# Mixture-of-experts rows turned by the DMA engines instead of TensorE, as two 16-bit halves

## The chip, the cores and the metric

The kernel runs on one core of a Trainium2 chip. A core has TensorE (matrix products and transposes; its sequence of weight loads is listed apart, as PEld), VectorE (DVE), ScalarE (ACT), GpSimd (POOL) and SyncE (SP), which here does nothing but issue transfers; 16 DMA engines carry all transfers. The engines run their own instruction streams in order and wait for each other through semaphores. On-chip data lies in SBUF (128 partitions); results of TensorE go to PSUM and are copied out by another engine. The metric is the device time of the whole program in microseconds (us), as the median of several runs.

## The reference

The input x is 2 x 2048 tokens of 512 float32 values. With xn the layer-normalised x, the result is x + s * g, where

```python
xn = _layernorm(x, axis=-1)
s = _L0_attn_ref(xn, ...)       # normalise again, causal attention of one head, key size 512, plus xn
g = _silu(_L0_ffn_ref(xn, ...)) # 8 experts, the best 2 per token
# inside _L0_ffn_ref, with xf = xn as (4096, 512):
scores = xf @ gate_w.T + gate_b + bias
top_scores, top_idx = jax.lax.top_k(scores, TOP_K)
gates = jax.nn.softmax(top_scores, axis=-1)
h = jax.nn.silu(jnp.einsum('td,ehd->teh', xf, w1) + b1)   # hidden size 352
y = jnp.einsum('teh,edh->ted', h, w2) + b2
out = jnp.einsum('ted,te->td', y, comb)  # comb: the two gates of a token
```

## The kernel before, in words

The work is written in four stages; a scheduler then orders the instructions of each engine ahead of time, and pools of buffers decide when a buffer may be used again.

First stage, lines 139 to 283: eight blocks of four token tiles (128 tokens each). `prepare(b)` loads x, takes its statistics on VectorE, makes the twice-normalised z (line 224) and, in place, the normalised x (line 229), and stores the latter as rows of `xn_d` in DRAM (line 232). TensorE transposes z; VectorE and ScalarE make kT and zT from it, and eight columns of gate scores follow. `project(b)`, three blocks later, makes q and v and stores them through four staging buffers (lines 273 and 283). The x buffer has two copies, so the load of block b+1 needs the store of block b-1 to be done.

Second, `route()`: the top two experts of each token, and a list of slots. Each expert's tokens are padded to whole slot tiles of 128 rows; there are 71 of them (NS). `toki` has the token of each slot, `eidi` the expert of each slot tile. The last three projections run on TensorE beside and behind it.

Third, the expert stage, lines 482 to 573, which the change is about. For slot tile i: `fetch(i)` gathers 128 rows of 2 KB from `xn_d` by an indirect transfer of GpSimd (line 503). `turn(i)` transposes the four 128x128 blocks on TensorE into PSUM (line 513), and VectorE copies them to xT (line 515). `up(i)` multiplies with the expert's w1 (line 527, eight instructions), ScalarE copies h out (line 532), `turn_h(i)` transposes h (line 540) and ScalarE applies silu with the bias (line 542). `down(i)` multiplies with w2 (line 552, six instructions), VectorE copies y out (line 557), and SyncE stores it to `y_d` (line 558). The loop puts them in this order:

```python
for i in range(NS):
    if i + AHEAD < NS:
        fetch(i + AHEAD)
    up(i)
    if i + 1 < NS:
        turn(i + 1)
    if i:
        down(i - 1)
    turn_h(i)
```

Fourth, lines 577 to 710: causal attention over the stored q, k, v, the gather of each token's two rows of `y_d`, the gate and the output.

All plain transfers named here are issued by SyncE, in order: an issue that waits holds up those behind it. The built program also lets each of them wait for the completion of the one eight places before it.

Of the kernel before, what the change touches and what calls it, by code (L numbers as in the profile page):

```python
# [10 lines left out]
F32 = mybir.dt.float32  # L11
BF16 = mybir.dt.bfloat16
I32 = mybir.dt.int32
AF = mybir.ActivationFunctionType
ALU = mybir.AluOpType
AX = mybir.AxisListType
# [3 lines left out]
P = 128  # L20
# [5 lines left out]
def gated_attention_moe(  # L26
# [26 lines left out]
    nc = tc.nc  # L53
    B, S, D = x.shape
    E, _, H = w1_t.shape
    KEY = o_proj.shape[0]
    NT = B * S // P
    BT = 4
# [3 lines left out]
    ND = D // P  # L62
# [10 lines left out]

    dram = ctx.enter_context(tc.tile_pool(name="dram", bufs=1, space=DRAM))
    xn_d = dram.tile([NT * P, D], F32, name="xn_d")
    y_d = dram.tile([NS * P, D], F32, name="y_d")
    kt_d = [dram.tile([P, ND, TB], F32, name=f"kt_d{b}") for b in range(NB)]
    qt_d = [dram.tile([P, ND, TB], F32, name=f"qt_d{b}") for b in range(NB)]
    v_d = [dram.tile([P, BT, D], F32, name=f"v_d{b}") for b in range(NB)]
    xn_rows = xn_d.rearrange("(n p) d -> p n d", p=P)  # L80
    y_rows = y_d.rearrange("(n p) d -> p n d", p=P)

    const = ctx.enter_context(tc.tile_pool(name="const", bufs=1))

    ident = const.tile([P, P], F32, name="ident")
# [5 lines left out]
        out=keep, in_=keep, compare_op=ALU.is_ge, fill=-HUGE,  # L91
# [38 lines left out]
    psum = lambda st, **k: st.enter_context(tc.tile_pool(space=PSUM, **k))  # L130
# [70 lines left out]
    def prepare(b):  # L201

        if b + 1 < NB:
            load(b + 1)
        xt = xin.pop(b)
        mv = sm.tile([P, BT, 2], F32, name=f"mv_{b}", tag="mv")  # L210
        for t in range(BT):
            st = sm.tile([P, 6], F32, name=f"st_{b}_{t}", tag="st")
            nc.vector.bn_stats(st, xt[:, t, :])
            nc.vector.bn_aggr(mv[:, t, :], st)
        va = sm.tile([P, BT, 2], F32, name=f"va_{b}", tag="va")
        nc.vector.tensor_scalar(va[:, :, 0:1], mv[:, :, 1:2], EPS, None, ALU.add)
        nc.vector.tensor_scalar(
            va[:, :, 1:2], mv[:, :, 1:2], 1.0 + EPS, EPS * EPS, ALU.mult, ALU.add
        )
        rs = rstd_of(sm, va, 2, "a")  # L220
        zs = []
        for t in range(BT):
            z = zp.tile([P, D], F32, name=f"z_{b}_{t}", tag="z")
            nc.vector.tensor_scalar(
                z, xt[:, t, :], mv[:, t, 0:1], rs[:, t, 1:2], ALU.subtract, ALU.mult
            )
            zs.append(z)
        for t in range(BT):
            nc.vector.tensor_scalar(
                xt[:, t, :], xt[:, t, :], mv[:, t, 0:1], rs[:, t, 0:1], ALU.subtract, ALU.mult  # L230
            )
        nc.sync.dma_start(out=xn_rows[:, ts(b, BT), :], in_=xt)

        ratio = sm.tile([P, BT], F32, name=f"ratio_{b}", tag="ratio")
        nc.vector.tensor_tensor(ratio, va[:, :, 1], rs[:, :, 1], ALU.mult)
        nc.vector.tensor_tensor(ratio, ratio, rs[:, :, 0], ALU.mult)

        zT = ztp.tile([P, ND, TB], F32, name=f"zT_{b}", tag="zT")
        kT = kp.tile([P, ND, TB], F32, name=f"kT_{b}", tag="kT")
        for c in range(ND):  # L240
            pt = ps_t.tile([P, TB], F32, name=f"pz_{b}_{c}", tag="pt")
            for t in range(BT):
                nc.tensor.transpose(pt[:, ts(t, P)], zs[t][:, ts(c, P)], ident)  # L243
            nc.scalar.copy(zT[:, c, :], pt)
            nc.vector.tensor_scalar(
                kT[:, c, :], pt, gam[:, c : c + 1], bet[:, c : c + 1], ALU.mult, ALU.add
            )
        nc.sync.dma_start(out=kt_d[b], in_=kT)
        kts[b] = kT
        pg = ps_g.tile([P, BT, E], F32, name=f"pg_{b}", tag="pg")  # L250
        for t in range(BT):
            for c in range(ND):
                nc.tensor.matmul(  # L253
                    pg[:, t, :], lhsT=zT[:, c, ts(t, P)], rhs=gw[:, c, :],
                    start=(c == 0), stop=(c == ND - 1),
                )
        nc.vector.tensor_tensor(
            sc[:, :, ts(b, BT)], pg.rearrange("p t e -> p e t"),
            ratio.unsqueeze(1).to_broadcast([P, E, BT]), ALU.mult,
        )  # L260
# [219 lines left out]


    with ExitStack() as st:
        xsp = st.enter_context(tc.tile_pool(name="xsp", bufs=4))
        xtp = st.enter_context(tc.tile_pool(name="xtp", bufs=2))
        hp = st.enter_context(tc.tile_pool(name="hp", bufs=2))
        yp = st.enter_context(tc.tile_pool(name="yp", bufs=3))
        htp = st.enter_context(tc.tile_pool(name="htp", bufs=1))
        hts = []
        for i in range(3):
            ht = htp.tile([P, NH, P], F32, name=f"ht_{i}", tag=f"ht_{i}")  # L490
            nc.gpsimd.memset(ht[HL : HL + 1, NH - 1, :], 1.0)
            hts.append(ht)
        stage_a.close()
        ps_x = psum(st, name="ps_x", bufs=2)
        ps_h = psum(st, name="ps_h", bufs=2)
        ps_ht = psum(st, name="ps_ht", bufs=2)
        ps_y = psum(st, name="ps_y", bufs=2)

        xss, xts, hs, experts = {}, {}, {}, {}

        def fetch(i):
            xs = xsp.tile([P, D], F32, name=f"xs_{i}", tag="xs")
            nc.gpsimd.indirect_dma_start(  # L503
                out=xs, out_offset=None, in_=xn_d,
                in_offset=bass.IndirectOffsetOnAxis(ap=toki[:, i : i + 1], axis=0),
            )
            xss[i] = xs

        def turn(i):
            xs = xss.pop(i)  # L510
            px = ps_x.tile([P, ND, P], F32, name=f"px_{i}", tag="px")
            for c in range(ND):
                nc.tensor.transpose(px[:, c, :], xs[:, ts(c, P)], ident)  # L513
            xT = xtp.tile([P, ND, P], F32, name=f"xT_{i}", tag="xT")
            nc.vector.tensor_copy(xT, px)  # L515
            xts[i] = xT

        def up(i):
            ev = nc.values_load(
                eidi[0:1, i : i + 1], engines=[mybir.EngineType.PE], min_val=0, max_val=E - 1,  # L520
                skip_runtime_bounds_check_because="a sum of E comparisons, the first of them true, less one",
            )
            experts[i] = ev
            xT = xts.pop(i)
            ph = ps_h.tile([P, H], F32, name=f"ph_{i}", tag="ph")
            for c in range(ND):
                nc.tensor.matmul(  # L527
                    ph, lhsT=xT[:, c, :], rhs=w1[:, bass.ds(ev, 1), c, :].rearrange("p o h -> p (o h)"),
                    start=(c == 0), stop=(c == ND - 1),
                )  # L530
            h = hp.tile([P, H], F32, name=f"h_{i}", tag="h")
            nc.scalar.copy(h, ph)
            hs[i] = h

        def turn_h(i):
            h = hs.pop(i)
            ht = hts[i % 3]
            pht = ps_ht.tile([P, NH, P], F32, name=f"pht_{i}", tag="pht")
            for c, (h0, hn) in enumerate(HCH):
                nc.tensor.transpose(pht[:hn, c, :], h[:, h0 : h0 + hn], ident)  # L540
            for c, (h0, hn) in enumerate(HCH):
                nc.scalar.activation(  # L542
                    ht[:hn, c, :], pht[:hn, c, :], AF.Silu, bias=b1sel[:hn, c, i : i + 1]
                )

        def down(i):
            ht = hts[i % 3]
            ev = experts.pop(i)
            py = ps_y.tile([P, D], F32, name=f"py_{i}", tag="py")
            for c, (_, hn) in enumerate(HCH):  # L550
                k = hn + 1 if c == NH - 1 else hn
                nc.tensor.matmul(  # L552
                    py, lhsT=ht[:k, c, :], rhs=w2[:k, bass.ds(ev, 1), c, :].rearrange("p o d -> p (o d)"),
                    start=(c == 0), stop=(c == NH - 1),
                )
            y = yp.tile([P, D], F32, name=f"y_{i}", tag="y")
            nc.vector.tensor_copy(y, py)  # L557
            nc.sync.dma_start(out=y_rows[:, i, :], in_=y)

        AHEAD = 3  # L560
        for i in range(AHEAD):
            fetch(i)
        turn(0)
# [9 lines that stand above are left out]
        down(NS - 1)  # L573
# [181 lines left out]
```

## Time and profile before

| what | value |
|---|---|
| time, median of 3 runs | 1321.16 us (1318.1 to 1328.13) |
| span of the profiled execution | 1319.4 us |
| first gather issued | 280.6 us |
| first transpose of slot tiles (line 513) | 324.3 us |
| last store of y issued | 732.7 us |
| stores of y, 256 KB each, issue to landing | 2.0 us |
| gathers, 256 KB each, issue to landing (median) | 3.3 us |
| first and last load of x | 1.7 and 127.0 us |

The profile is one execution. Busy time of an engine counts its instructions other than waits and issues of transfers; a group line gives, for one line of the kernel and one kind of instruction, output<-input, the count, busy time in us, mean ns of one, and the idle time of that engine before it with what ended most of it. Busy times of TensorE's groups overlap a little, since its instructions are pipelined. The chain follows the work that ended last back through what released it.

### The profile page before, as it was taken

To read this page: it belongs to the slowest core of one execution; us is meant where nothing else is said; L and a number is where in the kernel's file an instruction comes from. 1 tells how busy PE (TensorE), PEld (TensorE's weight loads), DVE (VectorE), ACT (ScalarE), POOL (GpSimd) and SP (SyncE) were. 2 spreads that over 40 slices of the span, in tenths; PEclk is the share of its full clock that TensorE was granted. 3 is DMA by queue.
4 is the path that set the end of the run, shared out by engine and by line. 5 is a ranking of instruction groups with operands and counts; after the bars stand their busy time and mean duration, and the time that the engine had idled before them with its cause. 6 is when DMAs were issued, how large, how long until landed. Compare 5 with 4: busy or idle time off the path is not lost.

```text
span 1319.4 us, 11878 instructions
## 1 busy us (share of the span) xinstructions
PE 1231.6 (93%) x3973; PEld 647.2 (49%) x3973; DVE 558.4 (42%) x1046; ACT 231.6 (18%) x593; POOL 261.3 (20%) x258
## 2 busy tenths in 40 slices
PE   6899999999999999999999478999999988899997
PEld 2565555444555555555555234444444434444443
DVE  2666223940222222222222395655444786554521
ACT  1222212111222222222222111111111011111010
POOL 0000000010111111111110364423112464321101
PEclk9899999999999999999999788999999999999999
DMA  9697332122322222222221883323114644121000
GB/s 349 218 358 279 128 128 88 72 96 99 119 94 96 89 95 89 96 94 90 90 95 64 326 295 104 122 69 111 41 40 177 237 128 137 59 68 48 24 9 16
DMA packets 68490, 162.84 MB, mean 123 GB/s; under 512 B 8968, under 2 KB 13064, under 8 KB 64336
## 3 DMA queue, kind: packets, MB, share of 16 engines
q1 hardware_dynamic: 52432, 116.71, 24.4%
q0 software_dynamic: 10800, 35.40, 8.7%
q10 hardware_dynamic: 5200, 9.98, 2.2%
q8 instruction: 33, 0.54, 0.2%
q14 instruction: 25, 0.20, 0.1%
HBM read 101.51 MB, written 60.56 MB: 123 GB/s over the span
## 4 chain that ended last, share of the span: by engine, by line
PE 52%; issue 22%; DVE 13%; POOL 6%; DMA 4%; SPq 1%; ACT 1%; POOLq 0%; ACTq 0%; DVEq 0%
PE py L552 14%; PE ph L527 13%; PE pv L277 8%; PE pq L267 8%; DVE e L622 7%; POOL o L693 3%; PE px L513 2%; POOL g L623 2%; PE pg L253 2%; PE pht L540 2%; DVE g L615 1%; DVE g L614 1%; PE pz L243 1%; ACT e L620 1%; DMA x<-in_x_dram 1%
## 5 line engine op out<-in xcount | busy, mean ns | idle before, releaser
L685 PE MATMUL po<-v,pT 128*128 128x512 f32 x544 | 253.9, 615 | 43.5 <-DVE pT L677 33.3
L640 PE MATMUL ps<-k,q 128*128 128x512 f32 (+3 forms) x640 | 246.0, 537 | 6.3 <-issue 6.3
L552 PE MATMUL py<-w,ht 128*128 (+1 forms) x426 | 194.8, 593 | 0.5 <-ACT ht L542 0.5
L685 PEld LDWEIGHTS po<-v,pT 128*128 128x128 f32 x544 | 102.5, 196 | 170.5 <-issue 108.1
L527 PE MATMUL ph<-w,xT 128*128 x568 | 179.9, 460 | 0.4 <-DVE xT L515 0.4
L640 PEld LDWEIGHTS ps<-k,q 128*128 128x128 f32 x640 | 118.4, 195 | 123.6 <-issue 115.9
L503 POOL DMA_INDIRECT xs<-xn_d,toki x71 | 67.4, 950 | 423.8 <-PE px L513 349.5
L515 DVE COPY xT<-px 128x512 f32<-128x512 f32 x71 | 49.0, 692 | 217.1 <-PE px L513 217.1
L267 PE MATMUL pq<-kT,wqk 128*128 128x512 f32 x256 | 125.0, 626 | 0.0
L527 PEld LDWEIGHTS ph<-w,xT 128*128 128x128 f32 x568 | 102.3, 190 | 45.7 <-DVE xT L515 0.6
L277 PE MATMUL pv<-wvo,kT 128*128 128x512 f32 x256 | 115.1, 596 | 0.0
L552 PEld LDWEIGHTS py<-w,ht 128*128 128x128 f32 (+1 forms) x426 | 75.6, 191 | 68.8 <-issue 51.2
L557 DVE COPY y<-py 128x512 f32<-128x512 f32 x71 | 49.1, 692 | 137.8 <-PE py L552 137.8
L622 DVE RECIPROCAL e<-e 128x512 f32<-128x512 f32 x32 | 107.1, 3346 | 0.4
L542 ACT ACTIVATE ht<-pht,b1sel 128x128 f32<-128x128 f32 (+1 forms) x213 | 62.0, 362 | 198.4 <-PE pht L540 198.4
L693 POOL TENSOR_TENSOR o<-o,g 128x512 f32<-128x512 f32 x32 | 40.5, 1266 | 258.7 <-DVE o L692 254.9
L656 ACT ACTIVATE pr<-ps,nm 128x512 f32<-128x512 f32 (+2 forms) x80 | 49.0, 620 | 219.2 <-DVE nm L651 216.2
L608 POOL DMA_INDIRECT yg<-y_d,posi x64 | 68.9, 1076 | 67.5 <-DMA y_d<-y 36.9
L277 PEld LDWEIGHTS pv<-wvo,kT 128*128 128x128 f32 x256 | 46.9, 190 | 51.0 <-issue 50.9
L692 DVE SCALAR_TENSOR_TENSOR o<-po,ri,xn 128x512 f32<-128x512 f32 x32 | 23.6, 737 | 106.1 <-PE po L685 106.1
L267 PEld LDWEIGHTS pq<-kT,wqk 128*128 128x128 f32 x256 | 47.5, 200 | 42.6 <-issue 42.4
L620 ACT ACTIVATE e<-g 128x512 f32<-128x512 f32 x32 | 20.1, 629 | 263.3 <-DVE g L615 252.7
(128 smaller groups left out, 937.4 us busy)
## 6 DMA issues: line engine op xcount, KB each, us to landing
y_d<-y SPq DMA_DIRECT2D x71, 256.0 KB, 2.0
x<-in_x_dram SPq DMA_DIRECT2D x32, 256.0 KB, 6.3
xn_d<-x SPq DMA_DIRECT2D x8, 1024.0 KB, 5.5
kt_d<-kT SPq DMA_DIRECT2D x8, 1024.0 KB, 4.6
qt_d<-q SPq DMA_DIRECT2D x32, 256.0 KB, 2.4
v_d<-v SPq DMA_DIRECT2D x32, 256.0 KB, 2.3
xn<-xn_d SPq DMA_DIRECT2D x32, 256.0 KB, 2.7
xo<-in_x_dram SPq DMA_DIRECT2D x32, 256.0 KB, 4.6
```

The costliest lines, as they stand in the source:

```text
L267: nc.tensor.matmul(pq, lhsT=wqk[:, c, ts(r, P)], rhs=kT[:, c, :], start=(c == 0), stop=(c == ND - 1),)
L277: nc.tensor.matmul(pv, lhsT=kT[:, c, ts(t, P)], rhs=wvo[:, c, :], start=(c == 0), stop=(c == ND - 1),)
L503: nc.gpsimd.indirect_dma_start(out=xs, out_offset=None, in_=xn_d, in_offset=bass.IndirectOffsetOnAxis(ap=toki[:, i : i + 1], axis=0),)
L527: nc.tensor.matmul(ph, lhsT=xT[:, c, :], rhs=w1[:, bass.ds(ev, 1), c, :].rearrange("p o h -> p (o h)"), start=(c == 0), stop=(c == ND - 1),)
L542: nc.scalar.activation(ht[:hn, c, :], pht[:hn, c, :], AF.Silu, bias=b1sel[:hn, c, i : i + 1])
L552: nc.tensor.matmul(py, lhsT=ht[:k, c, :], rhs=w2[:k, bass.ds(ev, 1), c, :].rearrange("p o d -> p (o d)"), start=(c == 0), stop=(c == NH - 1),)
L557: nc.vector.tensor_copy(y, py)
L608: nc.gpsimd.indirect_dma_start(out=y, out_offset=None, in_=y_d, in_offset=bass.IndirectOffsetOnAxis(ap=posi[k][:, n : n + 1], axis=0),)
L622: nc.vector.reciprocal(e, e)
L640: nc.tensor.matmul(ps[:, :w], lhsT=qts[b][:, c, ts(t, P)], rhs=kts[first + j][:, c, :w], start=(c == 0), stop=(c == ND - 1),)
L685: nc.tensor.matmul(po, lhsT=turned[j][:, ts(i, P)], rhs=vs[first + j][:, i, :], start=(j == 0 and i == 0), stop=(j == len(widths) - 1 and ...
L693: nc.gpsimd.tensor_tensor(o, o, g, ALU.mult)
```

## The change: the transpose moves from TensorE to the DMA engines

The DMA engines can transpose[...], and the rows are float32. So a float32 row is treated as 512 pairs of 16-bit halves. In the first stage GpSimd splits each normalised tile into a row of 512 low halves and 512 high halves, and SyncE stores these rows in a second DRAM tensor, `xh_d`, beside `xn_d`, which the fourth stage still reads. The expert stage gathers from `xh_d`; SyncE then issues a transposing transfer from SBUF to SBUF, 128 rows of 1024 halves to 8 blocks of 128x128, and VectorE's copy, which before took the result from PSUM, puts the two halves of every value side by side again in xT. No bit is lost, so xT is the same as before. Four TensorE transposes per slot tile and their PSUM buffers go. The gather and its buffers are one deeper: 5 buffers for the rows and 5 for the transposed halves, and four tiles of look-ahead in place of three. The rest of the program is the same.

```diff
--- before.py
+++ after.py
@@ -11,6 +11,7 @@
 F32 = mybir.dt.float32
 BF16 = mybir.dt.bfloat16
 I32 = mybir.dt.int32
+U16 = mybir.dt.uint16
 AF = mybir.ActivationFunctionType
 ALU = mybir.AluOpType
 AX = mybir.AxisListType
@@ -73,11 +74,14 @@
 
     dram = ctx.enter_context(tc.tile_pool(name="dram", bufs=1, space=DRAM))
     xn_d = dram.tile([NT * P, D], F32, name="xn_d")
+
+    xh_d = dram.tile([NT * P, 2 * D], U16, name="xh_d")
     y_d = dram.tile([NS * P, D], F32, name="y_d")
     kt_d = [dram.tile([P, ND, TB], F32, name=f"kt_d{b}") for b in range(NB)]
     qt_d = [dram.tile([P, ND, TB], F32, name=f"qt_d{b}") for b in range(NB)]
     v_d = [dram.tile([P, BT, D], F32, name=f"v_d{b}") for b in range(NB)]
     xn_rows = xn_d.rearrange("(n p) d -> p n d", p=P)
+    xh_rows = xh_d.rearrange("(n p) d -> p n d", p=P)
     y_rows = y_d.rearrange("(n p) d -> p n d", p=P)
 
     const = ctx.enter_context(tc.tile_pool(name="const", bufs=1))
@@ -230,6 +234,14 @@
                 xt[:, t, :], xt[:, t, :], mv[:, t, 0:1], rs[:, t, 0:1], ALU.subtract, ALU.mult
             )
         nc.sync.dma_start(out=xn_rows[:, ts(b, BT), :], in_=xt)
+        for t in range(BT):
+            xh = zp.tile([P, 2, D], U16, name=f"xh_{b}_{t}", tag="xh", bufs=2)
+            nc.gpsimd.tensor_copy(
+                xh, xt[:, t, :].bitcast(U16).rearrange("p (d h) -> p h d", h=2)
+            )
+            nc.sync.dma_start(
+                out=xh_rows[:, b * BT + t, :], in_=xh.rearrange("p h d -> p (h d)")
+            )
 
         ratio = sm.tile([P, BT], F32, name=f"ratio_{b}", tag="ratio")
         nc.vector.tensor_tensor(ratio, va[:, :, 1], rs[:, :, 1], ALU.mult)
@@ -480,7 +492,7 @@
 
 
     with ExitStack() as st:
-        xsp = st.enter_context(tc.tile_pool(name="xsp", bufs=4))
+        xsp = st.enter_context(tc.tile_pool(name="xsp", bufs=5))
         xtp = st.enter_context(tc.tile_pool(name="xtp", bufs=2))
         hp = st.enter_context(tc.tile_pool(name="hp", bufs=2))
         yp = st.enter_context(tc.tile_pool(name="yp", bufs=3))
@@ -491,7 +503,6 @@
             nc.gpsimd.memset(ht[HL : HL + 1, NH - 1, :], 1.0)
             hts.append(ht)
         stage_a.close()
-        ps_x = psum(st, name="ps_x", bufs=2)
         ps_h = psum(st, name="ps_h", bufs=2)
         ps_ht = psum(st, name="ps_ht", bufs=2)
         ps_y = psum(st, name="ps_y", bufs=2)
@@ -499,20 +510,22 @@
         xss, xts, hs, experts = {}, {}, {}, {}
 
         def fetch(i):
-            xs = xsp.tile([P, D], F32, name=f"xs_{i}", tag="xs")
+            xs = xsp.tile([P, 2 * D], U16, name=f"xs_{i}", tag="xs")
             nc.gpsimd.indirect_dma_start(
-                out=xs, out_offset=None, in_=xn_d,
+                out=xs, out_offset=None, in_=xh_d,
                 in_offset=bass.IndirectOffsetOnAxis(ap=toki[:, i : i + 1], axis=0),
             )
-            xss[i] = xs
+            xh = xsp.tile([P, 2 * ND, P], U16, name=f"xhT_{i}", tag="xhT")
+            nc.sync.dma_start_transpose(out=xh, in_=xs)
+            xss[i] = xh
 
         def turn(i):
-            xs = xss.pop(i)
-            px = ps_x.tile([P, ND, P], F32, name=f"px_{i}", tag="px")
-            for c in range(ND):
-                nc.tensor.transpose(px[:, c, :], xs[:, ts(c, P)], ident)
+            xh = xss.pop(i)
             xT = xtp.tile([P, ND, P], F32, name=f"xT_{i}", tag="xT")
-            nc.vector.tensor_copy(xT, px)
+            nc.vector.tensor_copy(
+                xT.bitcast(U16).rearrange("p c (t h) -> p c t h", h=2),
+                xh.rearrange("p (h c) t -> p c t h", h=2),
+            )
             xts[i] = xT
 
         def up(i):
@@ -557,7 +570,7 @@
             nc.vector.tensor_copy(y, py)
             nc.sync.dma_start(out=y_rows[:, i, :], in_=y)
 
-        AHEAD = 3
+        AHEAD = 4
         for i in range(AHEAD):
             fetch(i)
         turn(0)
```

## The prediction

> **What bounds the kernel now.** I began with the page's busy times and slices. TensorE is the engine to ask about, and the slices say where it is not full:
>
> ```profile
> PE 1231.6 (93%) x3973; PEld 647.2 (49%) x3973; DVE 558.4 (42%) x1046; ACT 231.6 (18%) x593; POOL 261.3 (20%) x258
> ...
> PE   6899999999999999999999478999999988899997
> ...
> DMA  9697332122322222222221883323114644121000
> ```
>
> A slice is 33 us. The expert stage (line 503 to 558) fills slices 10 to 21, at 9 throughout. The busy times by stretch, at edges of my choosing, say the same in microseconds. Columns: stretch, its length, busy time and count of PE, PEld, DVE, ACT and POOL, then granted clock, DMA share, GB/s.
>
> ```profile
> 0.00:60.00 60.00, 44.56 (x130) 23.71 (x131) 24.96 (x78) 9.41 (x18) 2.94 (x24) 0.91 0.80 279
> 60.00:110.00 50.00, 50.00 (x254) 33.03 (x253) 34.98 (x87) 13.28 (x26) 0.00 (x0) 1.00 1.00 352
> ...
> 330.00:725.00 395.00, 395.00 (x1453) 230.27 (x1452) 95.48 (x138) 92.68 (x280) 61.56 (x65) 1.00 0.28 92
> ```
>
> Two facts matter: in the expert stage TensorE never rests while VectorE is busy 24% and the DMA engines 28%; and between 60 and 110 us the DMA engines are full. So I took the chain that ended last, cut to 700 to 712 us, for one expert tile in order of time (start, length, line):
>
> ```profile
> 700.17 0.33 PE pht L540 x3
> 700.50 2.37 PE ph L527 x8
> 702.87 0.44 PE px L513 x4
> 703.30 2.58 PE py L552 x6
> 705.88 0.33 PE pht L540 x3
> 706.21 2.37 PE ph L527 x8
> ```
>
> The chain is TensorE and nothing else, with a period of 706.21 - 700.50 = 5.71 us. Of it the four transposes that the change removes take 0.44 us, not the 4 x 273 ns of their group line, since they overlap. Lastly I read the groups of what surrounds them:
>
> ```profile
> L503 POOL DMA_INDIRECT xs<-xn_d,toki x71 | 67.4, 950 | 423.8 <-PE px L513 349.5
> L515 DVE COPY xT<-px 128x512 f32<-128x512 f32 x71 | 49.0, 692 | 217.1 <-PE px L513 217.1
> ...
> L557 DVE COPY y<-py 128x512 f32<-128x512 f32 x71 | 49.1, 692 | 137.8 <-PE py L552 137.8
> ```
>
> All wait for TensorE; the gathers have 4.8 us of idle time each.
>
> **What the Trainium skill says.** VectorE: DVE Perf Modes, "The three transpose paths", gives 1309 ns for one 128x128 two-byte block through the DMA crossbar; no row of this trace shows a DMA transpose. DMA: Bandwidth & Descriptors, "Latency and other measured facts", gives 261 GB/s for one measured kernel and 350 to 400 GB/s for contiguous data; the nearest row here is the 256 KB store of y, 2.0 us to landing. GPSIMD Engine Reference, "Elementwise — side-by-side cycle accounting", has 512 elements in 769 ns at best; the trace has a two-input operation of 512 elements at 1266 ns (line 693). SBUF — State Buffer, "Who interferes with whom", says that GpSimd and a VectorE operation in two-port mode shut each other out; the trace has no GpSimd arithmetic in the first stage to test it.
>
> **Removed.** 71 tiles x 0.44 us = 31.2 us of the path. At the stage's start TensorE also waited 0.77 us for the first transpose and 0.40 us for the first xT (lines 513 and 527); both end, as xT is made long before: 1.2 us.
>
> **Added in the expert stage, per tile of 5.71 - 0.44 = 5.27 us.** (a) One DMA transpose of 128x1024 two-byte elements, 256 KB, on SyncE's queue. Low end: 256 KB at 261 GB/s, an estimate of 1.0 us, plus about 2 us of latency as for y. High end: eight 128x128 blocks at 1309 ns with no overlap, 10.5 us. The first price contains fixed cost that one instruction pays once, so I take 2 to 4 us. What decides is not latency but rate: it must be under 5.27 us per tile. For latency there is room. In the built order of SyncE's queue the transpose of tile i+9 stands behind the store of y(i), and its result is first read after y(i+5): five tiles, 26 us. Behind it waits the store of y(i+1), which has three buffers. It waits itself for the gather (3.3 us to landing in this trace) and for the VectorE copy of tile i+4, which comes straight after the copy of y(i). So this is hidden at my value. (b) The VectorE copy, now 1024 two-byte elements: 692 ns if bytes count, 2 x 692 = 1384 ns if elements do; I take 1.2. With y's 692 ns VectorE is busy 1.9 to 2.1 of 5.27 us: hidden under TensorE. (c) The gather moves rows of the same 2 KB: nothing. (d) The DMA share of 0.28 over 5.71 us is 1.6 us; with 1.0 us more it is about half: hidden. (e) The fifth buffer and the longer look-ahead only give slack. Before the stage, seven transposes stand among the last stores of q and v, and the first waits for the first gather, at 280.6 us; ScalarE fills these stores' four buffers every 3.43 us, so a stop of some 10 us costs nothing.
>
> **Added in the first stage.** 32 GpSimd copies of 1024 elements: 1.5 us each from twice 769 ns (2 x 1266 = 2.5 at worst), so 6 to 10 us per block of four, on an engine that is empty there. Then 32 stores of 256 KB, 8.4 MB. Two of these wait behind one another: xh has two buffers, so the third copy waits for the first store to land (3 to 6 us in the full stretch), SyncE waits for that copy, and the x loads of the block after next are queued behind it. Before, the loads of block 2 were issued at 38.8 us and those of block 3 from 65.3; I expect each 3 to 5 us later. In the first 60 us TensorE has idle time already (44.6 of 60 busy), so a late z there is paid in full; after 60 us it is always fed and prepared blocks run ahead. If every byte were exposed it would be 8.4 MB at 352 GB/s, 24 us; if none, 0. I take 5 us, with the shared port in it.
>
> **Sum.** 1321.2 - 31.2 - 1.2 + 5 = 1294 us, 2.1% faster.
>
> **The rivals.**
> Main case, 0.66: transposes stay under 5.27 us and hide. For it: DMA share 0.28, 26 us of slack. 1294, spread 1284 to 1306 by the first stage.
> Rival 1, 0.24: the DMA transpose becomes the bound, and TensorE waits for xT in every tile, VectorE's y copies queueing behind. For it: the only price of a whole transpose gives 10.5 us when multiplied, and all stand in one queue in order. Against it: the quoted bandwidth leaves a factor of four. At the middle of 5.27 and 10.5, 7.9 us, the stage takes 71 x (7.9 - 5.71) = 155 us longer: 1321 + 155 + 5 = 1481; at 10.5 us 1321 + 340 + 5 = 1666; at 6 us 1347.
> Rival 2, 0.10: the gain is real but the first stage gives it back. For it: DMA full from 60 to 110 us, x loads behind the new waits. Against it: TensorE has a backlog there. With all 24 us exposed: 1321.2 - 32.4 + 24 = 1313, within 1%.
>
> **How the numbers follow.** Faster by over 1% (under 1308) is the main case less a little for its upper tail: 0.65. Within 1%: rival 2 and the mildest of rival 1, 0.11. Slower: 0.24. The range starts at 1284, the sum with no cost in the first stage less a few us for a better start of the stage; upward it takes in rival 2 and a transpose just over 5.71 us, to 1345. What is left out is most of rival 1, two in ten.
>
> **What would show it.** Right: the period of line 527 in the expert stage falls to about 5.27 us, TensorE at 100% there, no wait of ph for xT, transposes landing in under 10 us. Stage one: q and v tiles shifted by 3 to 8 us. Wrong: TensorE waiting for xT tile after tile, VectorE's copy waiting for the DMA, the transpose queue taking most of 16 engines' time (rival 1); or TensorE idle between 40 and 110 us with VectorE waiting for x (rival 2). The weakest step is the rate of the transpose, for which I have no row; next is the start, where two buffers tie SyncE to GpSimd.

## The result, and the profile after

| | before | after |
|---|---|---|
| time, median of 4 runs | 1321.6 us (1318.1 to 1328.13) | 1302.33 us (1300.4 to 1304.12) |
| span of the profiled execution | 1319.4 us | 1300.5 us |
| first up-projection of the expert stage | 325.8 us | 340.2 us |
| first to last start of an up-projection | 399.5 us | 369.4 us |
| from there to the end | 594.1 us | 590.9 us |

The ratio of after to before is 0.985, interval 0.981 to 0.989. The three lower rows split the span in three, and their differences are +14.4, -30.1 and -3.2 us, together -18.9. The last is no finding: that part took 588 to 596 us over all kernels below. So the expert stage gives 30 us, and half of it is lost before that stage begins.

The page of the kernel after: busy times, TensorE's slices, its granted clock and the DMA share in slices of 33 us, and four groups.

```profile
PE 1210.1 (93%) x3689; PEld 622.2 (48%) x3689; DVE 572.3 (44%) x1046; ACT 231.1 (18%) x593; POOL 300.4 (23%) x290
...
PE   6998999999999999999999578999999979999997
...
PEclk9987999999999999999999789999999999999999
DMA  9897734119356656555642974222125643211000
...
L514 POOL DMA_INDIRECT xs<-xh_d,toki x71 | 71.5, 1007 | 364.0 <-DMA xhT<-xs 280.3
L525 DVE COPY xT<-xhT 128x1024 uint16<-128x1024 uint16 x71 | 49.8, 701 | 182.6 <-PE ph L540 164.2
...
L570 DVE COPY y<-py 128x512 f32<-128x512 f32 x71 | 49.1, 692 | 139.9 <-PE py L565 139.9
...
L239 POOL COPY xh<-x 128x1024 uint16<-128x1024 uint16 x32 | 35.2, 1121 | 163.8 <-DMA xh_d<-xh 85.3
```

In nine slices of the expert stage the DMA share has risen from 2 tenths to 5 and 6, and TensorE's slices there are still nines. The new VectorE copy waits for TensorE (164.2 of its 182.6 us: it waits until an up-projection frees an xT), for a transpose only twice, at the very start; in the gathers' group the transposes end the idle time, because a gather may now go out only when a transpose has emptied a row buffer, but no wait of TensorE comes of it. The last line has the new tie of the first stage: GpSimd's copies wait 85.3 us for their own stores. The fourth slice of PEclk is new too: 0.7, against 0.9 before.

Busy times by stretch of the kernel after, at the edges and in the columns used for the kernel before:

```profile
0.00:60.00 60.00, 45.36 (x147) 23.46 (x148) 27.59 (x67) 10.84 (x20) 10.91 (x31) 1.00 0.88 312
60.00:110.00 50.00, 43.59 (x185) 26.99 (x184) 34.91 (x86) 9.42 (x20) 11.80 (x11) 0.80 0.97 347
...
330.00:725.00 395.00, 386.45 (x1236) 214.19 (x1235) 97.50 (x140) 98.17 (x289) 63.70 (x63) 0.99 0.55 143
```

The first minute is no worse. The stretch that held 50.0 of 50 us of TensorE work now holds 43.6, at a granted clock of 0.80 instead of 1.00. The last stretch has its idle time almost all at the end: the stage ends earlier and 330 to 725 us now takes in the change of stages, where the first score matmul waits 7.4 us for its q (in the kernel before there is a wait of 6.3 us at this place, which the profile puts down to nobody).

The chain that ended last, two expert tiles between 652 and 662 us:

```profile
652.04 2.58 PE py L565 x6
654.62 0.33 PE pht L553 x3
654.95 2.37 PE ph L540 x8
657.31 2.58 PE py L565 x6
659.89 0.33 PE pht L553 x3
```

The 0.44 us of transposes are gone and nothing has come in their place: the period is 657.31 - 652.04 = 5.27 us.

What the moved work costs, from the view of the one tile xhT (duration in ns as minimum, median, maximum; on SyncE's queue this is the issue; the last line is the way to landing):

```profile
L519 SPq DMA_TRANSPOSE xhT<-xs x71: 1232/1232/3657, 300.3 to 673.9; - x71
L525 DVE COPY xT<-xhT x71: 694/695/941, 305.4 to 699.6; 128x1024 uint16<-128x1024 uint16 x71
...
DMA to landing us min/median/max: 3.0/3.6/5.2
```

A landing of 3.6 us against a period of 5.27: the transposes keep up even if no two overlap.

Where the first stage loses time, from TensorE's timeline of the kernel after between 90 and 111 us (in brackets the idle time before an instruction and what ended it):

```profile
90.73 1.07 PE L255 MATMUL pz<-ident,z 128*128 128x128 f32 x8
92.04 3.56 PE L265 MATMUL pg<-gw,zT 128*128 128x8 f32 x28 [0.24 <-ACT zT L256]
101.16 1.96 PE L255 MATMUL pz<-ident,z 128*128 128x128 f32 x8 [5.56 <-DVE z L228]
103.64 1.08 PE L265 MATMUL pg<-gw,zT 128*128 128x8 f32 x4 [0.52 <-ACT zT L256]
104.61 6.17 PE L289 MATMUL pv<-wvo,kT 128*128 128x512 f32 x8
```

TensorE waits 5.56 us for the z of block 4, while eight products of v stand behind it. TensorE works in the order in which the program was built, and the scheduler made another one than in the kernel before. There ten products of v fill this time:

```profile
91.20 2.96 PE L253 MATMUL pg<-gw,zT 128*128 128x8 f32 x26
94.02 4.54 PE L277 MATMUL pv<-wvo,kT 128*128 128x512 f32 x10
98.39 0.38 PE L243 MATMUL pz<-ident,z 128*128 128x128 f32 x2
```

VectorE makes the z of block 4 only 3.5 us later than in the kernel before, which has the first of these lines:

```profile
97.02 1.91 DVE L224 TENSOR_SCALAR z<-x,mv,rr_a 128x512 f32<-128x512 f32 x4
100.47 1.91 DVE L228 TENSOR_SCALAR z<-x,mv,rr_a 128x512 f32<-128x512 f32 x4
```

So the gap has two sides, a late z and an order that leaves nothing ahead of it. The x of that block came later still. SyncE's queue in the kernel before has this load at 78.4 us:

```profile
78.36 7.76 SPq L152 DMA_DIRECT2D x<-in_x_dram  x4
```

and in the kernel after at 86.4, behind new stores and what these hold up:

```profile
73.46 1.65 SPq L242 DMA_DIRECT2D xh_d<-xh  x2
...
76.31 0.48 SPq L260 DMA_DIRECT2D kt_d<-kT  x1
...
85.21 1.11 SPq L242 DMA_DIRECT2D xh_d<-xh  x2
86.41 4.33 SPq L156 DMA_DIRECT2D x<-in_x_dram  x4
```

Around the gap the clock is low. The two stretches of 20 us of the kernel before:

```profile
80.00:100.00 20.00, 20.00 (x88) 11.86 (x87) 15.49 (x47) 4.48 (x10) 0.00 (x0) 1.00 1.01 354
100.00:120.00 20.00, 20.00 (x79) 11.36 (x78) 14.10 (x39) 5.00 (x10) 0.00 (x0) 1.00 0.79 284
```

and of the kernel after:

```profile
80.00:100.00 20.00, 15.26 (x68) 9.27 (x66) 15.16 (x38) 2.56 (x6) 6.00 (x6) 0.84 1.00 353
100.00:120.00 20.00, 18.32 (x65) 11.51 (x66) 11.90 (x28) 4.34 (x9) 2.41 (x3) 0.67 0.87 299
```

TensorE's idle time ahead of the expert stage went from 18.2 to 23.4 us, the mean clock there from 0.97 to 0.94. So some 5 of the 14.4 us are idle time, and the other 9 are TensorE working longer on the same work: the mean q matmul takes 640 ns instead of 626, v 614 instead of 596.

### The profile page after: what moved, and what is told of

It reads as the page before. It is cut to its first block, busy times and chain, and to the rows that moved or that the text cites. A ratio compares the mean times of both kernels' runs of the same rounds, so it can differ in the third digit from the quotient of the medians.

```text
span 1300.5 us, 11587 instructions
## 1 busy us (share of the span) xinstructions
PE 1210.1 (93%) x3689; PEld 622.2 (48%) x3689; DVE 572.3 (44%) x1046; ACT 231.1 (18%) x593; POOL 300.4 (23%) x290
## 2 busy tenths in 40 slices
DMA packets 148074, 189.83 MB, mean 146 GB/s; under 512 B 84456, under 2 KB 88552, under 8 KB 143920
## 4 chain that ended last, share of the span: by engine, by line
PE 51%; issue 23%; DVE 14%; POOL 6%; DMA 4%; SPq 1%; ACT 1%; POOLq 0%; ACTq 0%; DVEq 0%
PE py L565 14%; PE ph L540 13%; PE pv L289 9%; PE pq L279 8%; DVE e L635 7%; POOL o L706 3%; PE pg L265 2%; POOL g L636 2%; PE pht L553 2%; DVE g L628 2%; DVE g L627 1%; PE po L698 1%; PE pz L255 1%; DVE mx L661 1%; SPq L190 1%
## 5 line engine op out<-in xcount | busy, mean ns | idle before, releaser
L514 POOL DMA_INDIRECT xs<-xh_d,toki x71 | 71.5, 1007 | 364.0 <-DMA xhT<-xs 280.3
L525 DVE COPY xT<-xhT 128x1024 uint16<-128x1024 uint16 x71 | 49.8, 701 | 182.6 <-PE ph L540 164.2
L565 PEld LDWEIGHTS py<-w,ht 128*128 128x128 f32 (+1 forms) x426 | 81.0, 191 | 83.7 <-issue 67.1
L289 PE MATMUL pv<-wvo,kT 128*128 128x512 f32 x256 | 118.9, 614 | 0.0
L555 ACT ACTIVATE ht<-pht,b1sel 128x128 f32<-128x128 f32 (+1 forms) x213 | 61.9, 361 | 167.8 <-PE pht L553 167.8
L239 POOL COPY xh<-x 128x1024 uint16<-128x1024 uint16 x32 | 35.2, 1121 | 163.8 <-DMA xh_d<-xh 85.3
```

Source lines behind the costliest of these rows:

```text
L289: nc.tensor.matmul(pv, lhsT=kT[:, c, ts(t, P)], rhs=wvo[:, c, :], start=(c == 0), stop=(c == ND - 1),)
L514: nc.gpsimd.indirect_dma_start(out=xs, out_offset=None, in_=xh_d, in_offset=bass.IndirectOffsetOnAxis(ap=toki[:, i : i + 1], axis=0),)
L525: nc.vector.tensor_copy(xT.bitcast(U16).rearrange("p c (t h) -> p c t h", h=2), xh.rearrange("p (h c) t -> p c t h", h=2),)
L555: nc.scalar.activation(ht[:hn, c, :], pht[:hn, c, :], AF.Silu, bias=b1sel[:hn, c, i : i + 1])
L565: nc.tensor.matmul(py, lhsT=ht[:k, c, :], rhs=w2[:k, bass.ds(ev, 1), c, :].rearrange("p o d -> p (o d)"), start=(c == 0), stop=(c == NH - 1),)
```

## The experiments

The theory at this point: the transposes are hidden and worth what was forecast; the loss lies in the first stage alone, and it comes from the two xh buffers, by which SyncE waits for GpSimd and GpSimd for SyncE's stores (the tie). Its rivals: the 8.4 MB of extra stores in a stage whose DMA engines are full; GpSimd's copies hindering VectorE at their shared port; a cost of the transposes that the chain doesn't show. For each run the profile gives when the expert stage starts, TensorE's idle time and clock before that, and when the x of block 4 is issued (before: 325.8 us, 18.2 us, 0.97, 78.4 us; after: 340.2 us, 23.4 us, 0.94, 86.4 us). Ratios are to the kernel before on the same chip, with their intervals.

### Split after the gather, so that the first stage is as before

```diff
-        # first stage: split into xh, store to xh_d
+            xs = xsp.tile([P, D], F32, ...)        # gathered from xn_d, as before
+            xl = xsp.tile([P, 2, D], U16, tag="xl")
+            nc.gpsimd.tensor_copy(xl, xs.bitcast(U16).rearrange("p (d h) -> p h d", h=2))
             xh = xsp.tile([P, 2 * ND, P], U16, tag="xhT")
-            nc.sync.dma_start_transpose(out=xh, in_=xs)
+            nc.sync.dma_start_transpose(out=xh, in_=xl.rearrange("p h d -> p (h d)"))
```

> The first stage is as in the kernel before (no 16-bit rows there); float32 rows are gathered and GpSimd splits each gathered tile into halves (1.04 us a copy) ahead of the transposing transfer. Theory (the 14.5 us by which the expert stage starts later, 340.2 against 325.8 us, come from the copies and stores added to the first stage): start of the expert stage back at about 325 us, period 5.28 us kept, about 1302 - 14.5 = 1288 us. Rival (the late start comes from the transposes that stand among the last stores of q and v, or from the larger buffers): start stays near 340 us and the time near 1302 us.

Measured: 1286.37 us (1283.16 to 1290.87), 0.973 [0.971, 0.976], faster than both kernels. The expert stage starts at 324.5 us, with 17.1 us of idle time and a clock of 0.97, and x of block 4 is issued at 79.5. The starts of the up-projections span 369.2 us, as after. The group of the copy on this kernel's page:

```profile
L508 POOL COPY xl<-xs 128x1024 uint16<-128x1024 uint16 x71 | 73.8, 1043 | 189.3 <-DMA xhT<-xl 183.5 <-DMA xs<-xn_d,toki 5.6
```

71 copies of 1.04 us on an engine that otherwise waits for buffers: no cost that shows. There is no store of halves in this kernel, and TensorE's order ahead of the expert stage is again that of the kernel before. It follows that the loss before the expert stage comes from what the change adds to the first stage.

### The same without split and transpose

```diff
-            nc.gpsimd.tensor_copy(xl, xs ...)
-            nc.sync.dma_start_transpose(out=xh, in_=xl ...)
-            xss[i] = xh
+            xss[i] = xs
...
-            nc.vector.tensor_copy(xT.bitcast(U16)..., xh.rearrange(...))
+            nc.vector.tensor_copy(xT, xs.rearrange("p (c t) -> p c t", c=ND))
```

> The kernel with the late split, but without split and transposing transfer: VectorE copies the gathered rows straight to xT, so rows go untransposed into the experts and the output is not the reference's; all else is kept. It is the floor of the expert stage. If split and transposing transfers are fully hidden there: within 3 us of the 1286.4 us of the late split. If they cost something (contention of DMA, VectorE's copy, the start): up to 10 us faster, and the profile shows where.

Measured: 1287.18 us, 0.974 [0.971, 0.978]; the starts of the up-projections span 369.2 us again. (Rows go untransposed into the experts here, so the output is not the reference's; the work of TensorE is the same.) The stretch from 450 to 650 us with transposes (split after the gather):

```profile
450.00:650.00 200.00, 200.00 (x646) 111.42 (x645) 55.89 (x76) 49.93 (x151) 69.43 (x67) 1.00 0.63 142
```

and without any:

```profile
450.00:650.00 200.00, 200.00 (x646) 111.61 (x645) 42.50 (x76) 50.41 (x152) 35.41 (x38) 1.00 0.31 100
```

TensorE does the same 646 matmuls in both. The DMA share is 0.63 or 0.31, and it makes no difference to the time that these intervals could show: moving the transposes is worth all that removing them could be, to within some 5 us.

### Every transpose made twice

```diff
             nc.sync.dma_start_transpose(out=xh, in_=xs)
+            more = xsp.tile([P, 2 * ND, P], U16, tag="more")
+            nc.sync.dma_start_transpose(out=more, in_=xs)
```

> The changed kernel with every transposing transfer made twice, the second into a tile that nothing reads. If transposes are hidden with a wide margin (1.23 us of SyncE's time each, DMA share 0.55 in the expert stage): period stays 5.28 us, DMA share about 0.82, time within 4 us of 1302 us. If the margin is small (16 engines' time is near its end): TensorE waits for xT and the period rises above 5.5 us, time above 1318 us.

Measured: 1375.75 us, 1.040 [1.037, 1.043]; the period is 432.8 / 70 = 6.18 us, 0.9 more than after. The loss is there, but not from the engines' rate: the DMA share between 450 and 650 us is 0.69 and a transpose still lands in 3.1 us (median). The waits of this kernel between 380 and 700 us (engine and line, what ended the wait; total us, times, longest):

```profile
DVE y L572 <- DMA y_d<-y: 205.3, 39, 8.3
POOL xs L514 <- DMA xhT<-xs: 183.9, 30, 8.7
...
PE py L567 <- DVE y L572: 35.5, 20, 3.0
```

and those of SyncE's queue in the same stretch:

```profile
SPq L521 <- DMA xs<-xh_d,toki: 156.0, 45, 6.1
```

Gathers wait for row buffers that a transpose must free; SyncE stands 156 us at the second transpose for such a gather; the stores of y are queued behind it; VectorE's copies of y wait 205 us for their buffers, and TensorE for its PSUM. In this stretch TensorE never waits for xT. So by the waits of this trace the limit that one more transfer per tile runs into is the one queue in which transposes and stores stand in order; no run gave the stores a queue of their own to test it. How far from it the kernel with one transpose is, this doesn't say in microseconds; that it is on the free side, the run without transposes does.

### Eight xh buffers in place of two

```diff
-            xh = zp.tile([P, 2, D], U16, name=f"xh_{b}_{t}", tag="xh", bufs=2)
+            xh = zp.tile([P, 2, D], U16, name=f"xh_{b}_{t}", tag="xh", bufs=8)
```

> The changed kernel with 8 buffers for the split rows in place of 2. Theory A (the third copy of a block waits for the first store to land, SyncE waits for the copy, and the x loads queue behind): the wait of the copies for stores of xh (85 us) falls to near 0, the 5.6 us stall of TensorE near 95 us goes, the granted clock between 60 and 110 us returns from 0.80 to near 1, and the time falls to 1290 to 1294 us. Theory B (8.4 MB more in a stretch where the DMA engines are full): the stall stays and the time stays within 3 us of 1302 us.

Measured: 1303.06 us, 0.985 [0.982, 0.988], the time of the kernel after. Expert stage at 343.8 us, idle time 26.3, clock 0.94, x of block 4 at 86.9. From this kernel's groups:

```profile
L239 POOL COPY xh<-x 128x1024 uint16<-128x1024 uint16 x32 | 37.0, 1195 | 157.6 <-DVE x L233 141.8 <-DMA xh_d<-xh 15.8
```

and from its waits ahead of the expert stage:

```profile
PE pz L255 <- DVE z L228: 5.3, 1, 5.3
```

The buffers did what they were given for, copies waiting for stores fell from 85.3 to 15.8 us; TensorE's gap of 5.3 us stayed. The tie as the one cause has fallen.

### The first stage's additions alone, and the copies alone

To the kernel before were added the declaration of xh_d and the loop of copies and stores, nothing in the expert stage; then the same loop without its store.

```diff
         nc.sync.dma_start(out=xn_rows[:, ts(b, BT), :], in_=xt)
+        for t in range(BT):
+            xh = zp.tile([P, 2, D], U16, name=f"xh_{b}_{t}", tag="xh", bufs=2)
+            nc.gpsimd.tensor_copy(xh, xt[:, t, :].bitcast(U16).rearrange(...))
+            nc.sync.dma_start(out=xh_rows[:, b * BT + t, :], in_=...)   # left out in the second kernel
```

> The kernel before with only the copies and stores of the split rows added to the first stage; nothing reads them, so the output is that of the kernel before. If the first stage alone costs the 14.5 us: about 1321 + 14.5 = 1336 us, with a stall of TensorE near 95 us. If the cost needs the transposes on SyncE's queue at the end of the second stage: within 4 us of 1321 us.

> The kernel before with the 32 GpSimd copies of the first stage alone, nothing stored. Theory port (GpSimd's copies hold the port that VectorE shares, so the preparation of blocks is late): 1330 us or more, as with copies and stores together (1334.8). Theory stores (their bytes, or their places on SyncE's queue): within 4 us of 1321 us, no stall of TensorE near 95 us.

Measured with copies and stores: 1334.83 us, 1.009 [1.007, 1.011]; expert stage at 345.8, idle time 27.3, clock 0.94, x of block 4 at 90.2. With copies alone: 1324.15 us, 1.002 [1.000, 1.004]; 330.8, 20.1, 0.97, 76.0. The copies alone cost 2 us by the medians, and the interval allows 0 to 6 us; most of the 12 to 13 us comes with the stores. But the copies do hinder VectorE. Its in-place normalisation in the kernel before, and with the copies alone:

```profile
L229 DVE TENSOR_SCALAR x<-x,mv,rr_a 128x512 f32<-128x512 f32 x32 | 15.3, 540 | 0.0
L233 DVE TENSOR_SCALAR x<-x,mv,rr_a 128x512 f32<-128x512 f32 x32 | 26.8, 897 | 0.0
```

The same 32 instructions take 897 ns instead of 540 (854 in the kernel after, 539 with the split after the gather). All of VectorE's work ahead of the expert stage takes 163.7 us instead of 145.8. VectorE has room for it here; but every kernel below with stores has the copies as well, and stores without copies were not tried. A cost that needs both is not excluded.

### Which side of the stores: bytes, places in the queue, buffers

Four kernels with the copies and another form of the stores, all without changes in the expert stage:

```diff
# short stores on SyncE, 64 of the 2048 bytes of each row
-                out=xh_rows[:, b * BT + t, :], in_=xh.rearrange("p h d -> p (h d)")
+                out=xh_rows[:, b * BT + t, 0:32], in_=xh[:, 0, 0:32]
# whole stores issued by GpSimd
-            nc.sync.dma_start(
+            nc.gpsimd.dma_start(
# each with two and with eight buffers
-            xh = zp.tile([P, 2, D], U16, ..., tag="xh", bufs=2)
+            xh = zp.tile([P, 2, D], U16, ..., tag="xh", bufs=8)
```

> Copies and the same 32 stores on SyncE, each of 64 bytes per row in place of 2048 (the rest is left out; nothing reads it). Theory bytes (8.4 MB more while the DMA engines are full): back to within 4 us of 1321 us. Theory queue (32 more issues in SyncE's order, each waiting for a copy and for the transfer eight places before): stays at 1330 us or more, with x loads of block 4 issued near 86 us instead of 78 us.

> Copies and full stores, the stores issued by GpSimd behind its copies and not by SyncE. Theory queue: back to within 4 us of 1321 us. Theory bytes: stays at 1330 us or more.

> The kernel before with copies and full stores, 8 buffers for the split rows, stores issued by GpSimd: the 8.4 MB are there, the tie of copy to store and the places on SyncE's queue are not. Theory late x (either of the tie or the queue makes the loads of x late, and that is what costs; the bytes do not): x of block 4 is loaded near 78 us, mean granted clock before the expert stage 0.97, expert stage starts near 326 us, about 1322 us. Rival bytes: x of block 4 at 85 us or later, 1330 us or more.

> The kernel before with copies, 8 buffers, and stores of 64 bytes per row on SyncE (the rest of each row is left out; nothing reads it): only the 32 places on SyncE's queue are there. Theory queue enough alone (as 8 buffers did not help the changed kernel): x of block 4 at 85 us or later and 1330 us or more. If it takes queue and bytes together: near 1322 us.

| stores | buffers | time, ratio [interval] | expert stage | idle time | clock | x of block 4 |
|---|---|---|---|---|---|---|
| short, SyncE | 2 | 1334.79, 1.009 [1.006, 1.012] | 342.7 | 21.2 | 0.94 | 85.3 |
| short, SyncE | 8 | 1329.87, 1.007 [1.004, 1.009] | 338.0 | 22.5 | 0.94 | 88.9 |
| whole, GpSimd | 2 | 1335.05, 1.010 [1.006, 1.014] | 340.7 | 21.5 | 0.94 | 86.9 |
| whole, GpSimd | 8 | 1336.2, 1.012 [1.009, 1.015] | 341.5 | 26.7 | 0.97 | 87.3 |

I had expected that one of these would be free. None is. The last has no added place in SyncE's queue and no copy that waits for a store, only bytes, and costs most, 16 us by the medians, where its expectation had 1322; the second has 1/32 of the bytes and no tie to speak of, only places in the queue, and costs 9.6, or some 6 more than the copies alone. Beside the copies each brings a loss, and the losses don't add up. The cleanest pair is whole stores by GpSimd with two buffers against copies alone: TensorE's, VectorE's, ScalarE's and SyncE's instructions stand in both in exactly the order of the kernel before, and the stores cost 1335.05 - 1324.15 = 10.9 us. So a new order is not needed for a loss. In the other three kernels of the table TensorE's order differs from that of the kernel before, as it does in the kernel after; what the order adds there, above all with places alone, was not separated.

One thing is common to all: the issue of x for block 4. In the kernel with only places (eight buffers):

```profile
88.89 4.90 SPq L156 DMA_DIRECT2D x<-in_x_dram  x4
```

with only bytes (whole stores by GpSimd, eight buffers):

```profile
87.28 3.48 SPq L156 DMA_DIRECT2D x<-in_x_dram  x4
```

with copies alone:

```profile
76.00 8.28 SPq L156 DMA_DIRECT2D x<-in_x_dram  x4
```

Every kernel that loses has it between 85 and 91 us, every one that doesn't at or before 80. With only bytes, SyncE stands 9.9 us before this load, until a store of x to `xn_d` has landed (longest such wait of a load in the kernel before: 4.8); with only places, the four short stores ahead of it take SyncE 9.6 us. The way to the delay is another one in each.

### A third x buffer

If late loads of x are the cause, a third x buffer should set them free. It was given to the kernel after, and to the one that splits after the gather.

```diff
-    xp = right(norm_a, name="xp", bufs=2)
+    xp = right(norm_a, name="xp", bufs=3)
```

> The changed kernel with three x buffers in place of two. Theory late x: x of blocks 2 and 3 is loaded ahead, TensorE's stall near 95 us goes, clock back to 0.97, 1289 to 1294 us. If the lateness comes from SyncE's order and not from the buffer, the x of block 4 stays late and the time stays near 1302 us.

> The late split with three x buffers, as a version: if the first stage is held by late x loads even there, TensorE's idle time before the expert stage (17 us with two buffers) falls and the time goes to about 1280 us; if not, within 3 us of 1286.4 us.

Measured: 1302.65 us, 0.986 [0.983, 0.988], and 1287.4 us, 0.975 [0.971, 0.979]: no gain in either. SyncE's queue in the first of the two:

```profile
42.60 3.11 SPq L156 DMA_DIRECT2D x<-in_x_dram  x5
...
86.79 4.74 SPq L156 DMA_DIRECT2D x<-in_x_dram  x4
```

The loads of block 3 came forward from 65 to 43 us, those of block 4 not at all: they are late for another reason than their buffer alone, and stand in the queue right behind two stores of halves (83.5 to 86.7 us). So this run did not move what it was meant to move, and the late x stays a companion of the loss, not a proven cause. In the second kernel block 4 was loaded from 61.9 to 76.5 us instead of 79.5 to 83.2 and the time stayed too, so an earlier load than that of the kernel before brings nothing that shows.

## Why the prediction was right, and where a term was wrong

**Direction and size.** 1294 us were forecast, 1302.3 measured. The gain was forecast as 27.4 us and was 19 us. Some 3 of these lie behind the expert stage, where no term forecast a gain and the kernels scatter by 8 us.

**Removed, 31.2 us.** Right. The period fell from 5.71 to 5.28 us, 30.1 us over 70 periods. The 1.2 us at the stage's start are not shown: the two waits are gone, but the first up-projection now waits 0.7 us for a copy of v by ScalarE. The kernel whose first stage is untouched starts the stage 1.3 us earlier than before, but the starts of such kernels scatter by more (319.5 to 324.5).

**The transposes' rate, called the weakest step.** Right, with a median of 3.6 us to landing in the 2 to 4 us taken (5.2 at most). Their share of the engines was underestimated: per tile the DMA engines were busy 0.28 x 5.71 = 1.6 us before and 0.60 x 5.28 = 3.2 us after, so one transpose of 256 KB costs some 1.6 us of all 16 engines, not 1.0 (1.7 by the runs with and without transposes, 1.4 by the doubled ones, with 6.7 us for a tile between 450 and 650 us); hence a share of 0.60 and not "about half". 256 KB in 1.6 us is 165 GB/s, an estimate from busy shares, below the 261 GB/s of the Trainium skill (DMA: Bandwidth & Descriptors, "Latency and other measured facts"). The high end, eight blocks at the 1309 ns of the skill's VectorE: DVE Perf Modes, "The three transpose paths", does not hold for one instruction over eight blocks: 10.5 us against 5.2 at most. How much of the 1309 ns is paid once, as the prediction assumed, no run with one block shows. With the high end Rival 1 fell. That the one queue and its order are a nearer limit than the engines' rate is what the waits with doubled transposes say.

**VectorE and GpSimd.** The interleaving copy takes 695 ns where 1.2 us were taken: for 1024 two-byte elements, what 512 float32 out of PSUM take (692). GpSimd's copies take 1.04 us at best instead of 1.5. The first is hidden, as forecast. What the prediction gives on the shared port and put into the 5 us agrees with the trace: VectorE's normalisation takes 897 ns instead of 540 beside the copies. No run shows that it is the port, but the copies are all that was added there; they cost 2 us by the medians, up to 6 by the interval.

**The last stores of q and v, at nothing.** Not seen to cost anything: with transposes and an untouched first stage the time is that of no transposes.

**First stage, 5 us.** This is the term that was mis-sized: 14.4 us in the profile, 12 to 13 us with these additions alone. The failed part is the sentence that after 60 us TensorE "is always fed and prepared blocks run ahead". It rested on 50.0 of 50 us busy, which says that TensorE had work, not how much was in store. The trace of the kernel before had the answer: VectorE began the z of block 4 at 97.0 us and TensorE took up its transposes at 98.4. Prepared blocks did not run ahead; projections of earlier blocks filled the time, by an order that the scheduler changed. Where the delay was looked for, there was little: block 2 was issued 3.0 us later, as forecast, and block 3 not later at all. And the loss is more than the gap: 5 us of idle time, and 9 us more of longer work at a lower granted clock. Whether the gap brings down the clock or both come from a third thing, no run separates; with only bytes added, the mean clock stayed at 0.97 and the loss came all the same.

How much goes with the clock can be estimated from runs of one kernel. In the 18 runs of the kernel before that stand beside the copies alone, the mean clock of the whole program goes from 0.982 (1315.8 us) to 0.971 (1331.8 us), and a line through all 18 falls by 1.3 us for each 0.001. The kernel after has a mean clock of 0.970, the one that splits late 0.977: by this rate about 10 of the 16 us between them go with the clock. With only bytes it is 0.975 against 0.977, about 3 of 16. This says what goes together, not what causes what.

**The step named as next weakest, the tie of two buffers.** As the one cause it fell with eight buffers. Beside the copies, bytes and queue places each bring the delay of block 4 and a loss. Which of the two acts in the kernel after, what TensorE's new order adds to it, and what brings down the clock stay open. Rival 2, the gain given back in the first stage, came half true: it gave back half. What the fifth row buffer and the longer look-ahead bring by themselves was not tried.

## What to carry to other kernels

A transpose can go from the engine that bounds a stage to idle DMA engines at no cost that shows, as long as the rate per tile and the room in its queue suffice; the run with the work left out gives the floor to compare with. The preparation that such a move needs belongs next to its use: split after the gather, the halves stay on the chip, while in the first stage they need 8.4 MB of stores on full DMA engines, and copies and stores cost 13 us. The better kernel takes 1286.4 us. A stretch at 100% busy says nothing of the work in store: look at how long before its use each input arrives, and at what the engine has ahead of it in its order.

## What the runs showed of the hardware

- One transposing transfer of 128x1024 two-byte elements from SBUF to SBUF: 1.23 us to issue on SyncE, 3.0 to 5.2 us to landing, 1.4 to 1.7 us of all 16 engines. It is cut small: the packets under 512 bytes of the program rose from 8968 to 84456, which is some 1,063 per transpose. Only two-byte elements were tried.
- With GpSimd's copies beside it, a VectorE normalisation of 128x512 float32 in SBUF takes 897 ns in the mean instead of 540, and GpSimd's copy 1.23 us (median) instead of 1.04 at best.
- Stores of 64 bytes per row in the full first stage (copies included) cost as much with two buffers as those of 2048, 13 us.
- Around a gap of 5.6 us of TensorE the granted clock was 0.84 and 0.67 in two stretches of 20 us, against 1.00 in both before. With only bytes added, the same two stretches have 2.2 and 4.4 us of idle time at 0.98 and 0.93: a gap and a low clock don't always come together.
